# Moving the transpositions of x and of the output ahead of the projections within each slice of a software-pipelined attention and convolution kernel

## The chip, the cores and the metric

The kernel runs on one core of one Trainium2 chip. The metric is the device time of one execution in microseconds. Before the change it is 5464.58 us, the median of three runs (5464.06 to 5466.99). The profile is of one execution with a span of 5462.3 us.

Engine names below are those of the profile: PE is the tensor engine (PEld its weight loads), DVE the vector engine, ACT the scalar engine, POOL the GpSimd engine, SP the queue that issues the transfers.

## The reference

Two layers work on x of shape 16 x 56 x 56 x 384 in fp32. Each normalises over 32 groups of 12 channels and adds its result to its input:

```
x = x + attention(group_norm(x))      # layer 0
x = x + binary_conv(group_norm(x))    # layer 1
```

The attention takes q, k and v from one 1 x 1 projection (3 x 384 by 384). It has 12 heads of 32 channels, in three groups of four heads with dilations 1, 2 and 3. Each pixel attends to the nine pixels of its dilated 3 x 3 neighbourhood: softmax over nine scores, a weighted sum of nine values, and a projection (384 by 384) with a bias. The convolution is depthwise, 3 x 3, with weights that are the signs of the given ones.

## The kernel before

An image is cut into seven chunks of 8 rows (448 pixels), so there are 112 chunks. All work between the ends is channel-major: 128 channels on the partitions, 448 pixels along the free dimension, and three such blocks for the 384 channels. Since x and the output are pixel-major in memory, both are turned with TensorE transpositions.

Three plans describe a chunk's work as small pieces:

- `plan_a` loads x, turns it (`turn(j)`, L378: four transpositions of 112 x 128 into a PSUM tile `pt_x`, copied by ACT at L382, statistics by DVE at L383) and stores it channel-major.
- `plan_b` is the attention. `k_or_v` (L416, PSUM tile `pkv`) and `query` (L416, PSUM tile `pq`) project, with three matmuls of 128 x 128 by 448 each, which the profile shows as six passes. `score` multiplies q with three shifted k on DVE (L466, tile `t`) and sums over the channels of a head on PE in rounds of four matmuls in 128 x 32 mode (L451, tile `ps`). `softmax_1` to `softmax_3` turn the scores (L486, tile `pt_s`), subtract the maximum (DVE, L491 and L492), take the exponential (ACT, L493) and normalise. `weigh` spreads the softmax weights over the channels of a head with three bf16 matmuls of 24 rows (L529, tile `pb_a`), multiplies with v on DVE (L536) and adds on POOL (L544 to L548). `out_project` (L562, tile `po`) projects, and DVE adds bias and residual (L565).
- `plan_c` is the convolution: normalisation on ACT (L639, L681), two blocks of channels on PE (L656, tile `pc`), the third on ACT and POOL (L703 to L717, or on DVE at L694 for the last image). `turn(s)` (L724, three transpositions into `pt_o`, copied by ACT at L726) turns the result, which L727 stores.

Every piece is filed with `at(when, order, piece)` under a slice and a rank within the slice. Chunk m of the attention begins at slice 9 m; x is nine chunks ahead of it and the output ten chunks behind. So nine slices are one step, in which each stage advances by one chunk. At the end the pieces are emitted sorted by slice, then rank. Per step, the slices hold, in that order on PE:

| slice | pieces on PE before the change |
|---|---|
| 0 | pt_s, pb_a, pkv, pkv, pt_x, pt_o |
| 1 | ps, pb_a, pt_o |
| 2 | ps, pc, pb_a, pq, pt_x, pt_o |
| 3 | ps, pb_a, pkv, pkv, pt_o |
| 4 | pb_a, pt_x |
| 5 | ps, pc, pb_a, pq |
| 6 | ps, pb_a, pkv, pkv, po |
| 7 | ps, pb_a, po |
| 8 | ps, pb_a, pq, po |

This emitted order is a priority. The framework's scheduler then fixes the order of every engine's instructions when the kernel is built, and there an instruction that is ready may be put ahead of one that isn't; on the chip each engine runs its list in that order.

The PSUM tiles pt_x, pkv, pt_s, po, pc, pt_o and those of the group statistics (pm, pb, pv, pp) share one pool of three banks (`ps_mt`, L85). A new tile takes a bank that was released: pkv, pt_x and pt_o are released by a copy on ACT, pt_s by the subtraction at L492, po by L565, pc by L663. The tile `pq` has a bank of its own, `ps` has one, and `pb_a` has three.

Of the kernel before, what the change touches and what calls it, by code (L numbers as in the profile page):

```python
# [35 lines left out]
def dilated_attention_then_binary_conv(  # L36
# [705 lines left out]
        for s in range(NSUB):  # L742
            at(t0 + 9 + s, STAGE_C, lambda s=s: turn(s))

    SOFTMAX, SCORE, STATISTICS, CONVOLVE, WEIGH, QUERY, QKV, PROJECT, STAGE_A, STAGE_C, NORM, LOADS = range(12)
    STEP = 9
    STAT0_SLICE = (0, 1, 2, 4, 5, 7)
    STAT1_SLICE = (0, 1, 2, 4, 4, 6)
# [35 lines left out]
```

## Time and profile before

| engine | busy us | share of the span | instructions |
|---|---|---|---|
| PE (matmul) | 5293.4 | 97% | 26901 |
| PEld (weight load) | 2335.4 | 43% | 26901 |
| POOL | 4212.5 | 77% | 3041 |
| DVE | 4157.7 | 76% | 4179 |
| ACT | 2412.6 | 44% | 4203 |

The rows of the table are the busy times of one execution. A matmul is pipelined, and the profile models its end, so the durations of matmuls that follow each other overlap: the time that a group of matmuls takes on PE is the distance from its first start to the first start of the next group.

The groups that the change moves, from the profile's list of groups (the count is of passes):

| group | passes | mean duration, ns |
|---|---|---|
| pkv, L416 | 4032 | 554 |
| pq, L416 | 2016 | 558 |
| po, L562 | 2016 | 551 |
| pt_x, L378 | 1344 | 268 (348 in the 48 passes of the first image's xin_z) |
| pt_o, L724 | 1344 | 280 to 287 |

### The profile page before, as it was taken

To read this page: it belongs to the slowest core of one execution; us is meant where nothing else is said; L and a number is where in the kernel's file an instruction comes from. 1 tells how busy PE (TensorE), PEld (TensorE's weight loads), DVE (VectorE), ACT (ScalarE), POOL (GpSimd) and SP (SyncE) were. 2 spreads that over 40 slices of the span, in tenths; PEclk is the share of its full clock that TensorE was granted. 3 is DMA by queue.
4 is the path that set the end of the run, shared out by engine and by line. 5 is a ranking of instruction groups with operands and counts; after the bars stand their busy time and mean duration, and the time that the engine had idled before them with its cause. 6 is when DMAs were issued, how large, how long until landed. Compare 5 with 4: busy or idle time off the path is not lost. (4 is left out here: it accounts for less than half of the span.)

```text
span 5462.3 us, 76025 instructions
## 1 busy us (share of the span) xinstructions
PE 5293.4 (97%) x26901; PEld 2335.4 (43%) x26901; DVE 4157.7 (76%) x4179; ACT 2412.6 (44%) x4203; POOL 4212.5 (77%) x3041
## 2 busy tenths in 40 slices
PE   6999999999999999999999999999999999999956
PEld 4443444444444444444444444444444444444422
DVE  3887778777777777777777778777777777877843
ACT  2223444444444444444444444544444444444433
POOL 1667788788888888888888888888888888888860
PEclk8999999999999999999999999999999999999975
DMA  5433556555555555555555555555555555545435
GB/s 165 131 105 107 153 159 166 159 156 156 157 159 160 158 159 164 155 158 158 160 164 155 160 160 159 162 158 158 155 157 157 161 161 159 160 133 135 129 93 140
DMA packets 833859, 827.88 MB, mean 152 GB/s; under 512 B 381379, under 2 KB 823238, under 8 KB 833478
## 3 DMA queue, kind: packets, MB, share of 16 engines
q1 hardware_dynamic: 825280, 817.58, 55.0%
q10 hardware_dynamic: 8198, 5.43, 0.3%
q8 instruction: 213, 3.49, 0.3%
q14 instruction: 168, 1.38, 0.1%
HBM read 468.47 MB, written 231.21 MB: 128 GB/s over the span
## 5 line engine op out<-in xcount | busy, mean ns | idle before, releaser
L544 POOL TENSOR_TENSOR w<-w 128x1344 f32<-128x1344 f32 x672 | 2049.9, 3050 | 516.2 <-DVE w L536 493.1
L466 DVE TENSOR_TENSOR t<-pq,k 128x1344 f32<-128x1344 f32 x1008 | 1535.6, 1550 | 247.7 <-PE pq L416 244.6
L416 PE MATMUL pkv<-xn,wqkvT 128*128 128x448 f32 x4032 | 1671.1, 554 | 1.3 <-ACT xa L382 1.2
L536 DVE TENSOR_TENSOR w<-pb_a,v 128x1344 f32<-128x1344 f32 x1008 | 1557.3, 1545 | 141.0 <-PE pb_a L529 74.7
L416 PEld LDWEIGHTS pkv<-xn,wqkvT 128*128 128x128 f32 x4032 | 719.9, 190 | 773.6 <-issue 727.5
L562 PE MATMUL po<-y,wprojT 128*128 128x448 f32 x2016 | 839.1, 551 | 36.1 <-POOL y L548 36.1
L416 PE MATMUL pq<-xn,wqkvT 128*128 128x448 f32 x2016 | 852.5, 558 | 0.0
L709 POOL TENSOR_TENSOR m<-m 128x1344 f32<-128x1344 f32 x210 | 639.3, 3044 | 216.0 <-ACT m L703 215.9
L639 ACT ACTIVATE z<-z,mrz 96x448 f32<-96x448 f32 x896 | 617.1, 751 | 361.4 <-DMA z<-x1d 310.9
L451 PE MATMUL ps<-t,sel 128*32 128x448 f32 x6048 | 751.9, 552 | 6.0 <-DVE t L466 6.0
L703 ACT ACTIVATE m<-zg,ktap 128x448 f32<-128x448 f32 x945 | 556.2, 657 | 292.0 <-POOL m L709 287.6
L656 PE MATMUL pc<-z,kdiag 96*32 96x440 f32 (+1 forms) x5376 | 578.5, 565 | 46.1 <-ACT z L639 26.7
L562 PEld LDWEIGHTS po<-y,wprojT 128*128 128x128 f32 x2016 | 375.2, 191 | 398.3 <-issue 345.0
L565 DVE SCALAR_TENSOR_TENSOR xr<-po,bias,xr 128x448 f32<-128x448 f32 x336 | 228.6, 680 | 369.3 <-PE po L562 369.2
L416 PEld LDWEIGHTS pq<-xn,wqkvT 128*128 128x128 f32 x2016 | 355.0, 190 | 328.9 <-issue 328.9
L663 DVE TENSOR_TENSOR x<-pc,x 128x448 f32<-128x448 f32 x224 | 139.8, 624 | 386.9 <-PE pc L656 386.9
L548 POOL TENSOR_TENSOR y<-y,w 128x448 f32<-128x448 f32 x336 | 382.5, 1138 | 23.4
L529 PE MATMUL pb_a<-aT,spread 24*128 24x448 bf16 x3024 | 383.3, 359 | 11.5 <-DVE w L536 11.2
L547 POOL TENSOR_TENSOR y<-w 128x448 f32<-128x448 f32 x336 | 382.3, 1138 | 13.8
L426 ACT COPY v<-pkv 128x448 f32<-128x448 f32 x336 | 179.6, 535 | 446.6 <-PE pkv L416 436.9
L382 ACT COPY xa<-pt_x 128x448 f32<-128x448 f32 x336 | 179.0, 533 | 399.3 <-PE pt_x L378 376.8
L426 ACT COPY k<-pkv 128x448 f32<-128x448 f32 x336 | 179.1, 533 | 391.9 <-PE pkv L416 391.3
(113 smaller groups left out, 4146.8 us busy)
## 6 DMA issues: line engine op xcount, KB each, us to landing
z<-x1d SPq DMA_DIRECT2D x608, 224.0 KB, 4.4
xn<-xd SPq DMA_DIRECT2D x112, 672.0 KB, 4.6
xr<-xd SPq DMA_DIRECT2D x112, 672.0 KB, 4.3
x1d<-xr SPq DMA_DIRECT2D x112, 672.0 KB, 3.2
out_dram<-osb SPq DMA_DIRECT2D x448, 168.0 KB, 2.9
xin<-in_x_dram SPq DMA_DIRECT2D x108, 672.0 KB, 7.0
xd<-xa SPq DMA_DIRECT2D x315, 224.0 KB, 3.1
x<-x1d SPq DMA_DIRECT2D x112, 448.0 KB, 8.2
```

Source lines behind the costliest of these rows:

```text
L416: nc.tensor.matmul(dst[:, :PX], wqkvT[:, cc, o0 : o0 + P], had["xn"][:, cc, :], start=(cc == 0), stop=(cc == NG - 1))
L451: return nc.tensor.matmul(had["ps"][32 * j : 32 * j + 32, :PX], sel[:, s0 : s0 + 32], tk, start=(i == 0), stop=(p + NQ >= NG * NTAP),)
L466: nc.vector.tensor_tensor(t.rearrange("p k (r w) -> p k r w", w=W), q3, k3, ALU.mult)
L529: return nc.tensor.matmul(pb[:, kx, :PX].rearrange("p (s n) -> p s n", s=NSUB), spread[rows_of, v % 2, :], had["a"][rows_of, :, v // 8, :] ...
L536: nc.vector.tensor_tensor(w.rearrange("p k (r w) -> p k r w", w=W), pb[:, :, :PX].rearrange("p k (r w) -> p k r w", w=W), three(kv[1][g][m ...
L544: nc.gpsimd.tensor_tensor(w0, w0, w, ALU.add)
L548: nc.gpsimd.tensor_tensor(y, y, w0[:, 2], ALU.add)
L562: nc.tensor.matmul(po[:, :PX], wprojT[:, g, j * P : (j + 1) * P], had[f"y{g}"], start=(g == 0), stop=(g == NG - 1))
L639: nc.scalar.activation(z[:, q], z[:, q], AF.Identity, bias=mrz[:, j, q, 0:1], scale=mrz[:, j, q, 1:2])
L656: return nc.tensor.matmul(pcr[q * HD : (q + 1) * HD, :, lo:hi], kdiag[:, kx, j * NQ + q, :], rows(z[:, q])[:, :, lo + kx - 1 : hi + kx - 1 ...
L703: nc.scalar.activation(rows(t[:, kx]), zp[:, ky : ky + ROWS, kx : kx + W], AF.Copy, scale=ktap[:, o : o + 1])
L709: nc.gpsimd.tensor_tensor(had["m"], had["m"], t, ALU.add)
```

## The change

Within a slice, the pieces that turn x (rank STAGE_A) and the output (rank STAGE_C) are emitted directly behind the piece that spreads the softmax weights (rank WEIGH), and so ahead of the query, key, value and output projections. Pieces stay in their slices. The aim is another order of TensorE's work: short transpositions behind the short spreading matmuls, and the long projections after both.

```diff
-    SOFTMAX, SCORE, STATISTICS, CONVOLVE, WEIGH, QUERY, QKV, PROJECT, STAGE_A, STAGE_C, NORM, LOADS = range(12)
+    SOFTMAX, SCORE, STATISTICS, CONVOLVE, WEIGH, STAGE_A, STAGE_C, QUERY, QKV, PROJECT, NORM, LOADS = range(12)
```

## The prediction

> **What bounds the kernel now.** I read the busy times first, then the row of forty slices, then the waits of TensorE (PE), then one step of the loop in order of time.
>
> ```profile
> PE 5293.4 (97%) x26901; PEld 2335.4 (43%) x26901; DVE 4157.7 (76%) x4179; ACT 2412.6 (44%) x4203; POOL 4212.5 (77%) x3041
> PE   6999999999999999999999999999999999999956
> PEclk8999999999999999999999999999999999999975
> ```
>
> PE is at 90% or more in all but the first and the last two slices, at the full clock. The busy time per stretch (the windows view) sharpens this: from 546 us to 5050 us PE is busy 100% of every stretch, and nearly all of its 169 us of idle time lies before 546 us and after 5187 us. A busy PE is a modelled thing, so I checked with start-to-start distances in one step of nine slices, from the timeline of PE:
>
> ```profile
> 2591.64 1.04 PE L486 MATMUL pt_s<-perm,sT 128*112 128x128 f32 x8
> 2592.61 0.36 PE L529 MATMUL pb_a<-aT,spread 24*128 24x448 bf16 x3
> 2592.91 4.78 PE L416 MATMUL pkv<-xn,wqkvT 128*128 128x448 f32 x12
> 2597.52 0.55 PE L378 MATMUL pt_x<-ident,xin 112*128 112x112 f32 x4
> 2597.90 0.38 PE L724 MATMUL pt_o<-ident,x 128*112 128x128 f32 x2
> ...
> 2598.33 0.96 PE L451 MATMUL ps<-t,sel 128*32 128x448 f32 x8
> 2599.22 0.36 PE L529 MATMUL pb_a<-aT,spread 24*128 24x448 bf16 x3
> 2599.51 0.43 PE L724 MATMUL pt_o<-ident,x 128*112 128x128 f32 x2
> ...
> 2603.11 0.36 PE L529 MATMUL pb_a<-aT,spread 24*128 24x448 bf16 x3
> 2603.40 2.52 PE L416 MATMUL pq<-xn,wqkvT 128*128 128x448 f32 x6
> 2605.76 0.55 PE L378 MATMUL pt_x<-ident,xin 112*128 112x112 f32 x4
> ...
> 2606.57 0.36 PE L529 MATMUL pb_a<-aT,spread 24*128 24x448 bf16 x3
> 2606.86 1.02 PE L416 MATMUL pkv<-xn,wqkvT 128*128 128x448 f32 x2
> 2607.81 0.96 PE L451 MATMUL ps<-t,sel 128*32 128x448 f32 x8
> 2608.70 4.03 PE L416 MATMUL pkv<-xn,wqkvT 128*128 128x448 f32 x10
> ```
>
> The next pt_s starts at 2637.47, so a step is 45.83 us; the following ones agree to 0.01 us. Nothing waits for data in it; every distance is a fixed cost of what stands next to what. So the time is what PE issues, plus what the neighbours cost, and a reordering can matter in two ways only: **other neighbours**, or **a wait that is not there now**.
>
> The neighbours, from the same step. Six po passes behind pq (2635.21 to 2637.47) take 2.26, or 0.376 a pass. Six pq passes behind pb_a take 2605.76 - 2603.40 = 2.36: **entering** a group with 128-column fp32 weights from pb_a costs 0.10 more. A pt_x group takes 0.38 behind pkv; behind pb_a, and followed by ps, 0.54 (2613.28 to 2613.82). Of these 0.16, 0.09 is the **exit** into another array mode (six po passes take 2.34 to 2.35 ahead of ps, against 2.26), so entering with pt_x costs about 0.06. In the same way pt_o takes 0.43 behind pt_x and 0.47 behind pb_a, both ahead of ps: its entry costs 0.05. The ten pkv passes behind ps take 3.87 = 10 x 0.376 + 0.11, so ps charges the entry of 0.10 as well.
>
> **What the Trainium skill says.** "TensorEngine Tiling (Array Packing)", Key Properties, has it that a change of tiling mode drains TensorE. The trace agrees: this is the exit of 0.09 between the 128-row groups and pb_a (24 rows) or ps (32 columns). "TensorE: Matmul & The Clock Gate", Step-by-step, lets weight loads run ahead of matmuls in flight while the matmuls keep their order; the 0.376 between pkv passes, with a new load each time, agrees. The same page, LDWEIGHTS, prices a load by its columns at P / 1.2: 107 ns for 128 columns, an estimate, close to the 0.10 that an entry exposes. "PSUM — Partial Sum Buffer", Engine vs sequencer instructions, calls the queue of ScalarE (ACT) strict FIFO; no wait in the trace contradicts it, and I need it for the rival.
>
> **The change, slice by slice.** It moves no work between slices; within one, the transpositions pt_x (slices 0, 2, 4) and pt_o (slices 0 to 3) now come before pq (2, 5, 8), pkv (0, 3, 6) and po (6 to 8). Only slices 0, 2 and 3 hold both kinds. No instruction is added or removed.
>
> Slice 2: pb_a, pq, pt_x, pt_o becomes pb_a, pt_x, pt_o, pq. The entry is paid by pt_x: 0.06 for 0.10, so **-0.04**. VectorE (DVE) gets pq about 0.8 us later (0.38 + 0.06 + 0.33) and its score product waits as long; behind it in DVE's queue are the weighing and the next product, but DVE is busy 35.98 of 45.83 us, and PE has twelve pkv passes of slice 3 (4.5 us) to run meanwhile, between which the ps round already lands today. I cost that wait at nothing.
> Slice 3: pb_a, pkv with a ps round inside, pt_o becomes pb_a, pt_o, pkv with ps inside: entry 0.05 for 0.10, **-0.05**.
> Slice 0 alike would give -0.04. Together **-0.13 us a step**.
>
> Unknown: the weights of pkv or pq behind a transposition, whose last pass streams only 0.11 us. No such pair exists now. The pt_s passes (112-column fp32 weights, same streaming of 128) stand 0.11 apart, so such a load just fits: lower end 0. Upper end: the load's own row says 190 ns on average, 0.08 more than 0.11, three times a step: +0.24. I take 0.
>
> **The new wait in slice 0.** All these groups share the three ps_mt banks. Now pkv follows pt_s and takes the banks of the last two po groups. After the change the sequence is pt_s, pt_x, pt_o, then v: pt_x and pt_o take those two banks, and v needs the bank of pt_s or of pt_x.
>
> ```profile
> 2592.53 0.68 DVE L565 SCALAR_TENSOR_TENSOR xr<-po,bias,xr 128x448 f32<-128x448 f32 x1
> 2593.12 0.60 DVE L491 TENSOR_REDUCE mx<-pt_s 112x48 f32<-112x432 f32 x1
> ...
> 2594.17 0.59 DVE L492 TENSOR_TENSOR ew<-pt_s,mx 112x432 f32<-112x432 f32 x1
> 2594.79 0.56 ACT L493 ACTIVATE ew<-ew 112x432 f32<-112x432 f32 x1 [3.90 <-DVE ew L492]
> ```
>
> The last po bank is free at 2593.21, just before pt_o wants it (2592.91 + 0.44 = 2593.35). The bank of pt_s is free only at 2594.76. That of pt_x: its last pass starts near 2593.26 and lasts 0.26, and ACT needs 0.53 to copy, so 2594.05 at best. PE is through with pt_o at 2593.68. So v is **0.4 to 1.1 us too early**. What fills this? The rows of slice 3 show the instruction order giving way to readiness: a ps round, first in the program order of its slice, stands after the first two pkv passes because its products were not ready. Here the ps round of slice 1 is ready: its product on DVE (2591.06 + 1.55) is done before pb_a. I expect it ahead of v: 0.89 us of work that covers the wait for the pt_x bank (0.09 + 0.89 after 2593.68 is 2594.66, against 2594.05). The price is one more change of mode: today pkv, pt_x, pt_o are one run between pb_a and ps; then pt_x and pt_o stand between pb_a and ps, and pkv between ps and pb_a. One more exit (0.09) and one more entry (0.10): +0.19. **The step gains 0.13 and pays 0.19: +0.06.**
>
> Sum: 93 of the 112 chunks have both transpositions beside them (x runs nine chunks ahead, the output ten behind): 93 x 0.06 = +5.6. The first ten, without pt_o, save 0.04 + 0.04 each, and the last nine, without pt_x, 0.05 x 3, both with banks to spare in slice 0: -2.3. Total +3.3 on 5464.6: **5468 us**. The ends of the run, where PE idles, hold the same work and I change nothing there.
>
> **The rivals.** *The saving comes through:* something else bridges the wait without a change of mode. 112 steps by 0.13 are -14.6: **5450**. For it: nothing else waits, every term is measured. Against: banks and copy times in slice 0, which leave 0.4 us even at best. *PE stands and waits,* because the order is fixed as if v were ready: with ACT's copy of pt_x prompt, 0.4 - 0.13 = +0.27, by 93: **5489**. With that copy queued behind the exponential (L493), which waits for DVE until 2594.79, v waits for the pt_s bank: 1.1 - 0.13 = +0.97, by 93: **5554**. For it: the queue of ACT is FIFO, and the exponential comes first in the program. Against: ACT stands idle 3.90 us there, time in which a ready copy would be placed. The weight loads at their upper end would add 93 x 0.24 = +22 to any of these.
>
> **How the numbers follow.** About flat (5468, give or take 8) 0.45; the saving 0.27; a standing PE 0.28, most of it near 5489. The range of 5446 to 5500 holds the flat case, nearly all of the saving and most of the short wait; it leaves out the long wait and loads at their worst. Faster by over 0.2% (below 5453.7): nearly all of the saving and a little of the flat case, 0.28. Slower by over 0.2% (above 5475.5): the waits and the flat case with dearer loads, 0.30. Within: 0.42.
>
> **What would show it.** In the timeline of the changed kernel, slice 0 should read pt_s, pb_a, pt_x, pt_o, ps, pkv x12, pb_a, and a step should last about 45.89 us. If pkv follows pt_o directly, the distance from pt_o to pkv tells the rivals apart: 0.11 is the saving (a step of 45.70), 0.5 or 1.2 the standing PE. From pt_o to pq in slice 2, 0.11 bears out the hidden load and 0.19 refutes it. I am wrong altogether if DVE or ACT falls behind over many steps, or if the order changes outside slices 0, 2 and 3.

## The result, and the profile after

The change makes the kernel **slower**: 5645.72 us (median of five runs, 5641.51 to 5648.54) against 5464.58, a ratio of 1.033 with a 95% interval of 1.0316 to 1.0344. The prediction was 5468 us, in a range of 5446 to 5500.

PE is no longer busy all the way. This is the row of the busy times of the kernel after, whose span is 5641.0 us. PE's idle time was 169 us before and is 5641.0 - 5328.4 = 313 us now.

```profile
PE 5328.4 (94%) x26901; PEld 2315.7 (41%) x26901; DVE 4164.3 (74%) x4179; ACT 2415.2 (43%) x4203; POOL 4207.4 (75%) x3041
```

The timeline of PE in one step of the kernel after (start, duration, line, tiles, count of passes, and in brackets the idle time before it with what ended it):

```profile
2534.83 1.04 PE L486 MATMUL pt_s<-perm,sT 128*112 128x128 f32 x8
2535.80 0.36 PE L529 MATMUL pb_a<-aT,spread 24*128 24x448 bf16 x3
2536.09 0.60 PE L378 MATMUL pt_x<-ident,xin 112*128 112x112 f32 x4
2536.53 0.38 PE L724 MATMUL pt_o<-ident,x 128*112 128x128 f32 x2
...
2536.95 0.96 PE L451 MATMUL ps<-t,sel 128*32 128x448 f32 x8
2537.84 4.78 PE L416 MATMUL pkv<-xn,wqkvT 128*128 128x448 f32 x12
2542.55 0.36 PE L529 MATMUL pb_a<-aT,spread 24*128 24x448 bf16 x3
...
2547.40 0.27 PE L724 MATMUL pt_o<-ident,xg 128*112 128x128 f32 x1
2547.51 2.42 PE L416 MATMUL pq<-xn,wqkvT 128*128 128x448 f32 x6
...
2550.43 0.27 PE L724 MATMUL pt_o<-ident,xg 128*112 128x128 f32 x1
2550.53 1.67 PE L416 MATMUL pkv<-xn,wqkvT 128*128 128x448 f32 x4
...
2556.53 0.60 PE L378 MATMUL pt_x<-ident,xin 112*128 112x112 f32 x4
...
2560.18 0.36 PE L529 MATMUL pb_a<-aT,spread 24*128 24x448 bf16 x3
2560.48 2.52 PE L416 MATMUL pq<-xn,wqkvT 128*128 128x448 f32 x6
2565.55 0.37 PE L529 MATMUL pb_a<-aT,spread 24*128 24x448 bf16 x3 [2.55 <-DVE w L536]
```

The first part, down to 2542.55, is slice 0, and its order is the one forecast: the ps round stands between pt_o and pkv. Slices 2 and 3, from 2547.40, also hold pt_o ahead of the projections, as intended. The last line is new. At the head of slice 6, in which no transposition was moved, pb_a waits 2.55 us for the weighing on DVE. From the waits of the whole execution (total us, times, longest):

```profile
ACT zg L681 <- DMA xg<-x1d: 346.3, 93, 7.4
DVE stats L383 <- ACT xa L382: 348.9, 107, 6.5
PE pb_a L529 <- DVE w L536: 143.2, 74, 3.3
```

Before, the three read 49.2, 49.3 and 11.2 us. They form a chain, which one step shows when it is read backwards, first on DVE, then on ACT, then on SP.

```profile
2556.70 1.56 DVE L536 TENSOR_TENSOR w<-pb_a,v 128x1344 f32<-128x1344 f32 x1 [0.78 <-POOL w L544]
2562.88 0.63 DVE L383 BATCH_NORM_STATS2 stats<-xa 128x6 f32<-128x448 f32 x1 [4.62 <-ACT xa L382]
2563.42 0.61 DVE L663 TENSOR_TENSOR x<-pc,x 128x448 f32<-128x448 f32 x1
2563.95 1.55 DVE L536 TENSOR_TENSOR w<-pb_a,v 128x1344 f32<-128x1344 f32 x1
```

The weighing at 2563.95 uses the pb_a that PE wrote at 2560.18, and yet DVE idles until 2562.88. Ahead of the weighing in DVE's list stand the statistics of the x transposition of slice 4, which wait for its copy xa. PE began that transposition at 2556.53; ACT copied it only at 2562.34:

```profile
2550.78 0.48 ACT L726 COPY osb<-pt_o 112x384 f32<-112x384 f32 x1 [2.49 <-issue]
2554.08 0.54 ACT L426 COPY v<-pkv 128x448 f32<-128x448 f32 x1 [2.82 <-PE pkv L416]
2559.33 0.85 ACT L681 ACTIVATE zg<-xg,mr 128x560 f32<-128x560 f32 x1 [4.71 <-DMA xg<-x1d]
2560.22 1.23 ACT L703 ACTIVATE m<-zg,ktap 128x448 f32<-128x448 f32 x2
2561.35 0.51 ACT L426 COPY k<-pkv 128x448 f32<-128x448 f32 x1
...
2562.34 0.51 ACT L382 COPY xa<-pt_x 128x448 f32<-128x448 f32 x1
```

ACT stood 4.71 us before zg, the normalisation that starts the next chunk's convolution on ACT and POOL, because the load of its input xg had not landed. Before the change, zg stands behind xa in ACT's list, as in the step that the prediction shows:

```profile
2613.93 0.53 ACT L382 COPY xa<-pt_x 128x448 f32<-128x448 f32 x1 [0.25 <-PE pt_x L378]
...
2617.91 0.86 ACT L681 ACTIVATE zg<-xg,mr 128x560 f32<-128x560 f32 x1 [0.74 <-DMA xg<-x1d]
```

Counted from the pt_s of its step, this xa begins at 22.3 us before (2613.93 - 2591.64) and at 27.5 us after (2562.34 - 2534.83). Of the 94 steps that hold both, zg is ahead of xa in 80 in the changed kernel, and in 1 before. The load went out late on SP:

```profile
2550.07 1.59 SPq L516 DMA_TRANSPOSE aT<-e  x1
2551.76 1.19 SPq L634 DMA_DIRECT2D z<-x1d  x1
2553.05 0.39 SPq L385 DMA_DIRECT2D xd<-xa  x1
2553.53 0.88 SPq L727 DMA_DIRECT2D out_dram<-osb  x2
2554.51 0.40 SPq L670 DMA_DIRECT2D xg<-x1d  x1
```

There are two xg buffers, and the last reader of one is the output transposition of slice 3. It now comes ahead of 4.5 us of pkv, so the buffer is free earlier. On the chip the load goes out some 4 us after that transposition (2550.5 to 2554.5), and zg begins 4.8 us after that, which is also the load's median time to land in this kernel (3.5 us before). Why zg moved up is my reading: when the kernel is built, the scheduler takes the load, and with it zg, for ready that much earlier, and fills a gap on ACT with zg. The scheduler's estimates are in no trace; what the experiments show is that the early transposition moves zg.

To split the loss: the 91 steps from the eleventh on took 4220.7 us before and 4393.5 after, so 173 of the 179 us between the two profiled spans arise there; the start is 5.6 us longer, the rest 0.3.

### The profile page after: what moved, and what is told of

Read it like the earlier page. It is cut to its first block, busy times and chain, and to the rows that moved or that the text cites. A ratio compares the mean times of both kernels' runs of the same rounds, so it can differ in the third digit from the quotient of the medians.

```text
span 5641.0 us, 76008 instructions
## 1 busy us (share of the span) xinstructions
PE 5328.4 (94%) x26901; PEld 2315.7 (41%) x26901; DVE 4164.3 (74%) x4179; ACT 2415.2 (43%) x4203; POOL 4207.4 (75%) x3041
## 5 line engine op out<-in xcount | busy, mean ns | idle before, releaser
L709 POOL TENSOR_TENSOR m<-m 128x1344 f32<-128x1344 f32 x210 | 639.3, 3044 | 198.0 <-ACT m L703 195.9
L451 PE MATMUL ps<-t,sel 128*32 128x448 f32 x6048 | 763.3, 560 | 5.5 <-DVE t L466 5.5
L703 ACT ACTIVATE m<-zg,ktap 128x448 f32<-128x448 f32 x945 | 569.8, 660 | 176.4 <-POOL m L709 171.8
L383 DVE BATCH_NORM_STATS2 stats<-xa 128x6 f32<-128x448 f32 x336 | 207.8, 619 | 349.0 <-ACT xa L382 348.9
L529 PEld LDWEIGHTS <-spread 24*128 24x128 bf16 x3024 | 113.0, 92 | 718.2 <-issue 658.7
L726 ACT COPY osb<-pt_o 112x384 f32<-112x384 f32 x448 | 213.4, 479 | 423.7 <-issue 260.2
```

The lines of the kernel that those rows point to most:

```text
L451: return nc.tensor.matmul(had["ps"][32 * j : 32 * j + 32, :PX], sel[:, s0 : s0 + 32], tk, start=(i == 0), stop=(p + NQ >= NG * NTAP),)
L529: return nc.tensor.matmul(pb[:, kx, :PX].rearrange("p (s n) -> p s n", s=NSUB), spread[rows_of, v % 2, :], had["a"][rows_of, :, v // 8, :] ...
L703: nc.scalar.activation(rows(t[:, kx]), zp[:, ky : ky + ROWS, kx : kx + W], AF.Copy, scale=ktap[:, o : o + 1])
L709: nc.gpsimd.tensor_tensor(had["m"], had["m"], t, ALU.add)
```

## The experiments

**Theory A** is the chain above: early pt_o in slice 3, early load and zg, ACT waits, DVE waits behind the statistics, PE waits. **Rival B**: the query of slice 2 comes 0.8 us later, which delays the score product, and DVE falls behind. Ratios are to the kernel before.

**x_early: only the transpositions of x early.**

```diff
-    ..., WEIGH, STAGE_A, STAGE_C, QUERY, QKV, PROJECT, NORM, ...
+    ..., WEIGH, STAGE_A, QUERY, QKV, PROJECT, STAGE_C, NORM, ...
```

> Only the transpositions of x come early (slices 0, 2, 4); those of the output stay behind the projections. Theory A (the early pt_o of slice 3 frees the buffer xg, the load of xg and its normalisation zg on ACT are placed ahead of the copies of k and xa, and ACT waits there for the load): xg is freed as before, zg stands behind xa, no wait; the entries save 0.04 us in slice 0 and 0.04 in slice 2, so 103 steps by 0.08 are -8: about 5456 us. Rival B (the score product on DVE gets the query of slice 2 late, and DVE falls behind): the query is 0.44 us late here, a bit over half of the 0.77 in the changed kernel, so the weighing of slice 5 is late again and a part of the loss stays: 5530 to 5600 us.

Measured: 5467.21 us, 1.0005 (0.9996 to 1.0014). There is no loss, though the query is late here as well: against B. The plain step is 45.755 us, which is the 0.08 less that was forecast. But the saving doesn't reach the total. In one step of seven a matmul of the group statistics (pv) takes a bank between pt_s and pt_x, and the step is 47.15 instead of 46.77; over 91 steps the time is 4220.7, as before. The start is 5.9 us longer and the end some 2.5 us shorter.

**s3_late: the change, with the fourth output transposition left behind the projections.**

```diff
-            at(t0 + 9 + s, STAGE_C, lambda s=s: turn(s))
+            at(t0 + 9 + s, LATE_C if s == NSUB - 1 else STAGE_C, lambda s=s: turn(s))   # LATE_C: behind PROJECT
```

> The change with one exception: the fourth output transposition, that of slice 3, stays behind the projections. Theory A: the wait of PE for the weighing at the head of slice 6 is gone; slice 0 costs 0.15 (one more change of mode less the cheaper entry; I had +0.06 in all with 0.05 back from slice 3 and 0.04 from slice 2), slice 2 gives 0.04: a step of 45.93 us, 5474 us. Rival B: the query of slice 2 is as late as in the changed kernel, so the loss stays: about 5640 us.

Measured: 5485.47 us, 1.0039 (1.0024 to 1.0054). The step is 45.93 us, as expected. The waits of this kernel:

```profile
DVE stats L383 <- ACT xa L382: 59.6, 28, 6.3
ACT zg L681 <- DMA xg<-x1d: 57.8, 59, 2.9
```

The query is as late as in the changed kernel, and the chain is gone: B falls. The 11 us over the forecast are the start (6.4 longer than before) and the steps with group statistics.

**s3_alone: the kernel before, with that one transposition early.**

```diff
-            at(t0 + 9 + s, STAGE_C, lambda s=s: turn(s))
+            at(t0 + 9 + s, EARLY_C if s == NSUB - 1 else STAGE_C, lambda s=s: turn(s))   # EARLY_C: behind WEIGH
```

> The kernel before with one piece moved: the fourth output transposition (slice 3) ahead of the projections. Theory A: the order on ACT is that of the changed kernel around zg, and the loss is there without any later query: steps of 46.8 to 50 us, 5464.6 - 5 + about 178 = 5638 us. Rival B: nothing is late, slice 3 saves 0.05 a step: 5460 us.

Measured: 5620.29 us, 1.0281 (1.0263 to 1.0298). One piece moved, with no query delayed, brings 156 of the 181 us, and with it the chain; these are its waits:

```profile
ACT zg L681 <- DMA xg<-x1d: 326.5, 93, 7.1
DVE stats L383 <- ACT xa L382: 317.7, 105, 8.8
PE pb_a L529 <- DVE w L536: 124.5, 73, 2.9
```

**zg_behind_xa: the changed kernel, with zg held behind xa on ACT.**

```diff
-            nc.scalar.copy(xa, pt[:, :PX])
+            last_xa[0] = nc.scalar.copy(xa, pt[:, :PX]).ins
...
+            with tc.issue_after(last_xa[0]):
                 nc.scalar.activation(zp[:, lo:hi, 1 : W + 1], ...)          # L681
```

> The changed kernel with one order fixed: the normalisation zg (L681) is issued on ACT behind the copy xa of slice 4. The early load of xg stays, the query is as late as in the changed kernel. Theory A: no wait at slice 6, a step of 45.88 us, 5468 us as first forecast. Rival B: the loss stays, 5640 us. Rival C (the load of xg itself, ahead of other transfers, holds something up): the loss stays as well, 5600 us or more.

Measured: 5465.29 us, 1.0002 (0.9993 to 1.001). The order of instructions on PE and on DVE is exactly that of the changed kernel, and the load of xg goes out as early. ACT's order differs, and with it the place of zg's sums (L709) on POOL, which follow zg. ACT still waits 129.1 us for the load, but now with xa behind it. The plain step is 45.875 us, and the wait of PE is back at the level of before:

```profile
PE pb_a L530 <- DVE w L537: 13.0, 9, 2.3
```

Rivals B and C fall, and zg's place on ACT is what costs the time; that for most of the loss it isn't POOL's order shows in stats_behind below. Over the 91 steps this kernel takes 4229.8 us: of the 173 us, 164 are waits and 9 the neighbours on PE. As PE's order is the same in both kernels, their traces can be compared matmul by matmul: 133 of the 164 us arise just ahead of pb_a at the head of slice 6, and nearly all the rest in slices 5 and 6.

**zg_alone: the same hold in the kernel before.**

```diff
+            with tc.issue_after(last_xa[0]):       # in the kernel before, and nothing else
```

> The kernel before with the normalisation zg (L681) issued on ACT behind the copy xa of slice 4, and nothing else. In the steady steps zg stands there already, so a step stays 45.83 us. Theory A1: the start gains, since in the run zg_behind_xa a step of the first images lasted 44.66 us where before has 54.39; that is 10 us from the order of zg and not from the transpositions: 5454 us, and the transpositions' order without its wait then costs 11 us. Theory A2: that gain belongs to the early transpositions: 5464 us.

Measured: 5454.47 us, 0.9982 (0.9975 to 0.9989). The steady part is unchanged (4220.5 us over the 91 steps), but the tenth step takes 44.79 instead of 54.34. This is A1: the total of zg_behind_xa, close to my 5468, holds a gain of some 10 us at the start that has nothing to do with the transpositions, so that it came close is luck. Against zg_alone their order costs 11 us, where I had forecast 3.

**slices_2_3: slice 0 as before, the rest early, zg held.** The first transposition of each kind keeps its old rank:

```diff
-            at(t0 + 2 * j, STAGE_A, lambda j=j: turn(j))
+            at(t0 + 2 * j, EARLY if j else STAGE_A, lambda j=j: turn(j))
...
-            at(t0 + 9 + s, STAGE_C, lambda s=s: turn(s))
+            at(t0 + 9 + s, EARLY if s else STAGE_C, lambda s=s: turn(s))   # EARLY: behind WEIGH; the rest behind PROJECT
```

> Slice 0 as before (projections first), slices 1 to 4 as changed, and zg issued behind xa. Theory A (entries as priced, no wait): slice 2 saves 0.04 and slice 3 0.05, a step of 45.74 us; 93 steps give -8, and the start is worth -10 where zg_alone shows it: 5446 us, or 5456 without it. Rival B (a query that comes late to DVE makes the weighing late): above 5475 us.

Measured: 5437.82 us, 0.9952 (0.994 to 0.9965): **faster than both kernels**. Its timeline of PE in slices 2 and 3:

```profile
2582.56 0.36 PE L530 MATMUL pb_a<-aT,spread 24*128 24x448 bf16 x3
2582.86 0.43 PE L726 MATMUL pt_o<-ident,x 128*112 128x128 f32 x2
...
2583.23 0.55 PE L379 MATMUL pt_x<-ident,xin 112*128 112x112 f32 x4
2583.62 2.43 PE L417 MATMUL pq<-xn,wqkvT 128*128 128x448 f32 x6
2585.98 0.36 PE L530 MATMUL pb_a<-aT,spread 24*128 24x448 bf16 x3
```

pb_a to the next pb_a is 3.42 us where it was 3.46 (2603.11 to 2606.57 before). The step is 45.73; 91 steps take 4212.2, or 8.5 less. Most of the rest comes from the start: the ninth and tenth step take 42.41 and 45.19 us, against 51.49 and 54.34. The tenth gains in zg_alone as well; why the ninth does, I haven't tested.

**stats_later and stats_behind: is it DVE that holds PE?** Both are the changed kernel with the statistics of slice 4 taken later, except in the last chunk of an image; the first only files them two slices later, the second also ties them behind the weighing of slice 6.

```diff
+        if c < NCH - 1:
+            at(t0 + 6, STAGE_A, lambda: statistics(NG - 1))      # instead of in turn(2)
...
+                tc.add_manual_dep(i.ins, last_w[0].name, NOSYNC)  # stats_behind alone
```

> The changed kernel, but DVE takes the statistics (L383) of the x transposition of slice 4 two slices later, except in the last chunk of an image. zg stays ahead of k and xa on ACT, so ACT still waits for the load. Theory A with its last link (DVE, in order, stands behind the statistics, which wait for xa, and the weighing of slice 5 behind them): PE's wait at slice 6 goes in six steps of seven, 5475 to 5500 us. Rival D (PE is held through the banks that ACT's late copies of k and xa keep, not through DVE): the loss stays, 5600 us or more.

Measured: 5644.06 us, 1.033 (1.0316 to 1.0344). The forecast missed, and the run tests nothing: a later slice is only a lower priority, and DVE's list still had the statistics ahead of the weighing.

> As stats_later, whose DVE order turned out to be unchanged (the statistics were ready early in the plan and filled a gap). Now the statistics (L383) of slice 4 are tied behind the weighing of slice 6 on DVE. On ACT zg stays ahead of xa as in the changed kernel, so ACT still waits for the load. Theory A with its last link (DVE stands behind the statistics): PE's wait at slice 6 goes in six steps of seven, 5475 to 5500 us. Rival D (PE is held through the banks that ACT's late copies keep): the loss stays, 5600 us or more.

Measured: 5546.48 us, 1.0146 (1.0129 to 1.0163). Between the two answers. The waits of stats_behind:

```profile
ACT zg L692 <- DMA xg<-x1d: 351.6, 93, 7.2
PE pb_a L540 <- DVE w L547: 33.7, 21, 2.3
```

ACT waits as long as in the changed kernel, and the orders of ACT and POOL are the changed kernel's but for two instructions on each. And yet PE's wait at pb_a falls from 143 to 34 us; many plain steps take 45.88 us. So the statistics in DVE's queue are the link for most of the loss. What stays is 81 us over the kernel before. More than half of it lies in the steps in which the last chunk of an image is turned (14 steps of 48.7 to 52.0 us, against 46.77 before), where the statistics are still early. Some 22 us are a new wait in slice 0, between pt_x and pt_o, mostly for the residual add on DVE. I haven't taken it further apart, so a part for Rival D isn't excluded.

**xg3: three buffers for xg**, in the changed kernel.

```diff
-    xg_p = ctx.enter_context(tc.tile_pool(name="xg_p", bufs=2))
+    xg_p = ctx.enter_context(tc.tile_pool(name="xg_p", bufs=3))
-            rest = s_p.tile([...], F32, tag="rest", name="rest")
+            rest = s_p.tile([...], F32, tag="sT", name="rest")
```

> The changed kernel with three buffers for xg instead of two (the softmax's tile rest shares a slot with sT to make room). The load of xg no longer waits for the last output transposition. zg still stands ahead of xa on ACT in most steps. Theory A: its data have landed long before, so ACT doesn't wait and DVE and PE don't either: steps of 45.9 us, 5470 us. If the place of zg on ACT is bad in itself (0.85 us of zg and the taps behind it ahead of k and xa), the loss stays in part: 5520 us or more.

Measured: 5774.74 us, 1.0575 (1.0559 to 1.0591). The clearest miss. With the buffer free still earlier, zg and its taps moved to slices 8 and 0, and the sums of the taps on POOL then stood before the softmax's own work there: in one step of this kernel, rest (L509) starts on POOL at 2754.54, behind three of them, though its input was there at 2751.87. ACT's wait for rest (at L510) is 355.4 us in all, against 147.2 before. The transposing transfer of the weights waits for that, and the loads behind it. That this is what costs the time isn't tested. As a test of A the run decides nothing, since it moved more than it was meant to; the shared slot of rest may add to it. It shows once more that an earlier buffer makes other engines' lists different.

**xg_on_act: the load of xg issued from ACT's queue**, in the changed kernel.

```diff
-            nc.sync.dma_start(
+            nc.scalar.dma_start(
                 xg[:, lo:hi, :].rearrange("p r w -> p (r w)"),
```

> The changed kernel with the load of xg issued from ACT's queue instead of SP's. In the changed kernel that load stands on SP behind the transposing transfer of the softmax weights, a z load and three stores, and goes out 4.0 us after the last output transposition (2550.5 to 2554.5). From ACT it goes out right behind the copy of that transposition, so it lands some 4 us earlier; zg stands even further ahead on ACT, before the copy of v. Theory A: ACT's wait for the load falls to what the load itself takes (3.5 to 5 us from the copy) and ends before pt_x of slice 4 is there, so xa is not late: 5470 to 5490 us. If the wait was the load's own length and not its place on SP: 5600 us or more.

Measured: 5489.99 us, 1.0045 (1.003 to 1.006). ACT still waits for the load (288.8 us in all), but earlier, and PE's wait at pb_a is down to 13.6 us: plain steps of 45.87 us. Here zg is ahead of xa in the same 80 steps as in the changed kernel. So the loss needs two things at once, zg ahead of xa on ACT and a load that goes out late on SP: zg_behind_xa takes the first away and wins back 180 us, this run the second and wins back 156.

## Why the prediction was wrong, step by step

- **PE is the bound, every distance is a cost of neighbours:** right.
- **The entries:** right. The step of 45.89 forecast for the change is 45.875 once the wait is gone (zg_behind_xa). The later forecasts, made with the changed kernel's trace at hand, were 45.75, 45.93 and 45.74; measured were 45.755 (x_early), 45.93 (s3_late) and 45.73 (slices_2_3).
- **The weight load behind a transposition, taken at 0 of 0 to +0.24:** right. In the kernel after, 2547.40 (the third pass of pt_o) to 2547.51 (pq) is 0.11 us.
- **The hoisted ps round in slice 0:** right in order and price. From pt_s to the pb_a of slice 1 it takes 7.72 us (2534.83 to 2542.55) against 7.58 before, and -0.04 + 0.19 = 0.15 were forecast. A standing PE in slice 0, my slow rival, didn't happen; the slow case came from elsewhere.
- **Slice 3, "-0.05":** this is the step that failed. I priced the earlier pt_o as a matter of PE alone and asked only what its PSUM bank waits for. I didn't ask what its *reading* releases: xg, whose next load and normalisation are on SP and ACT. The term that was left out, the wait for that load behind zg, is +1.8 us a step (164 us over 91 steps). Moved alone, this one piece costs 156 us (s3_alone); with it left in place, the change costs 21 (s3_late).
- **"It moves no work between slices":** true of the emitted list, wrong of the instruction lists. zg moved ahead of k and xa on ACT.
- **The FIFO of ACT:** I cited it for the exponential in slice 0, where the scheduler had put ready copies first, as I expected. The same FIFO did the damage with zg, whose input, as I read it, the scheduler took for landed.
- **The sum, +3.3:** too low even without the wait; the order costs 11 us against zg_alone, 9 of them over the 91 steps. I priced plain steps alone. Two of the seven steps of an image, with matmuls of the group statistics, lose more: 47.03 and 47.99 us in zg_behind_xa against 46.77 and 47.81. (The terms of the first ten and last nine chunks also add up to -2.15, not -2.3.)
- **The start:** wrong in small. I expected a saving of 0.08 us in each of the first ten steps; the changed kernel loses 5.6 us there. Why, I haven't tested.
- My closing condition, DVE or ACT falling behind over many steps, is what came true. I named it and gave it no time.

## What to carry to other kernels

When an instruction is moved, list what it frees as well as what it needs: every buffer that it reads last is the start of another load, and a scheduler that fills gaps may move that load's consumer too. On an engine that runs its list in order, an instruction that waits for a transfer must not stand ahead of copies that other engines need soon; tie it behind them by an explicit order. Check the order of all engines after a reordering, not only of the one that was reordered.

## What the runs showed of the hardware that I had not expected

The issue of transfers itself takes long on SP: in the kernel after, a median of 1.56 us for the transposing one (L516) and of 0.47 us for all others. Five of them about the release of the buffer, from 2550.07 to 2554.41, held its next load back by 4 us, nearly as much as that load's own median of 4.8 us.

TensorE's schedule repeats where nothing waits: 52 steps of the kernel before last 45.82 or 45.83 us, so differences of 0.04 us a step could be read.
